# Roots on GpSimd, a sigmoid made of tanh, and one reciprocal for two softmax sums in a two-layer gated transformer kernel

## The chip, the cores and the metric

The kernel runs on one core of one Trainium2 chip. A core has five engines that run at the same time, each with its own in-order instruction stream: TensorE (PE, matrix products; its weight loads, PEld, are shown apart), VectorE (DVE), ScalarE (ACT, which evaluates functions such as exp from tables), GpSimd (POOL) and SyncE (SP, which issues DMAs). They wait for each other on semaphores. The metric is the device time of one execution in microseconds, the median of several runs. Lower is better.

## The reference

The input is x (4 batches, 512 rows, 512 columns) and a context (4, 512, 128). Four residual blocks follow one another, each gated by the tanh of a scalar. Cut to what matters here:

```python
# block 1: a learned adjacency, from the context
sim = einsum('bhnd,bhmd->bnm', Q, K) / (sqrt(32) * 4)
threshold = top_k(sim, 153)[0][:, :, -1:]
A = sigmoid(sim) * (sim >= threshold)
A = (A + swapaxes(A, -1, -2)) * 0.5
gamma = sigmoid(gamma_raw)
x = x + tanh(g_xattn[0]) * ((1 - gamma) * layernorm(x) + gamma * A)
# block 2: ternary weights, 8-bit activations, Hadamard rotations
x = x + tanh(g_ffn[0]) * down(silu(gate(layernorm(x))) * up(layernorm(x)))
# block 3: 16 heads, latent keys from the context, rotary positions
attn = softmax(scores); x = x + tanh(g_xattn[1]) * attention(layernorm(x), context)
# block 4: root-mean-square norm, ternary weights, 8-bit activations
x = x + tanh(g_ffn[1]) * (h + out(value * silu(gate)))   # h = layernorm(x)
```

where `layernorm(x) = (x - mean) / sqrt(var + 1e-5)` over the columns, without weights.

## The kernel before, in words

Everything is tiled to 128 partitions. A batch is four row tiles of 128x512 (`xs[b, j]`), an intermediate of the feed-forward blocks is 128x2048 a row tile. Matrix products of the attention are in fp32; the feed-forward products multiply bf16 activations with fp8 ternary weights.

**Adjacency (block 1, `adjacency`, lines 395 to 458).** For each of a batch's four row tiles, PE makes the similarities, ACT scales them into `sim` (line 420), and DVE finds the 153rd largest value of each row: 20 rounds of the eight largest (`max`, line 426), with `match_replace` (line 428) striking them out of `work` between rounds. ACT takes the sigmoid of `sim` (line 433), and one DVE instruction compares `sim` with the threshold and multiplies by the sigmoid (line 434). After the four tiles come the layer norm's statistics and the sum with the transpose (lines 437 to 458), scaled by `c_new`.

**Roots (`rsqrt_cols`, lines 147 to 159).** The reciprocal root of 128x4 variances (one column for each row tile): DVE adds epsilon, ACT takes the root (line 153), DVE takes the reciprocal (line 154), and four small DVE instructions make one Newton step. `ln_stats` calls it for the norms ahead of blocks 1, 2, 3 and 4 of each batch, and `feed1` once more for the root-mean-square norm: 20 calls.

**Feed-forward (`feed0`, `feed1`, `gated`, `tiles`, `projected`).** Silu on ACT (line 296), its product with the other half on DVE (line 297), Hadamard butterflies (DVE in line 513, GpSimd in line 481), quantization, transposes on PE with copies on ACT, and the product with the second weights (line 386). The weights are made ternary on ACT (`ternary`, lines 204 to 241: Abs with a sum, then Identity and Sign). The second layer's weights are made while attention runs.

**Attention (class `Pair`, lines 712 to 828).** 16 heads are worked two at a time: 8 pairs for each of 4 batches. `head` makes queries, `rope` rotates them (products with cosine and sine on DVE, lines 745 to 750, their sum on GpSimd, line 751), `rotated` projects them (line 708). `scores(j)` handles one block of 128 rows of both heads: two score matrices in PSUM (lines 781 and 784), and for each head the negated row maximum on DVE (line 789), Exp with its row sum on ACT (line 792), the reciprocal of the sum on DVE (line 794) and the product with it on ACT (line 795). The sums and reciprocals are 128x1 tiles. `turn(j)` transposes the result on PE (line 803) and copies it to `pT` on ACT (line 804). `attended` and `added` multiply with the values (line 811) and the output weights (line 823) and add to x (line 828). Within a pair, `scores(j)` goes out beside the next pair's queries and `turn(j - 2)`; the last two blocks are turned at the end of the pair. `hidden_T` (lines 671 to 681) makes the normalized, transposed hidden state at the start of a batch's attention.

**What sets the order.** The source interleaves generators. `attention` yields once a row block; between two yields, pieces of the next batch's adjacency and first feed-forward block, or of the second layer's weights and feed-forward, are issued according to their estimated costs (the numbers behind `yield`) and due times (`jobs`, lines 931 and 932). From that order and the dependencies, the framework places each instruction on its engine's stream: an instruction whose inputs are expected later can be overtaken by a later one of the source. On the chip each stream is then in order. Tiles take their places from rotating pools (`bufs`). In front of an ACT instruction whose function isn't in the table set that is active, a table load is put into ACT's stream; these loads carry the line of the instruction behind them.

At the start, batch 0's adjacency runs with the preparation of keys and output weights (`ahead`, whose DMAs to device memory are issued from POOL's queue, lines 647 and 667) and of the first layer's weights. At the end, the last feed-forward runs without attention beside it (`alone`).

Of the kernel before, what the change touches and what calls it, by code (L numbers as in the profile page):

```python
# [9 lines left out]
F32 = mybir.dt.float32  # L10
# [5 lines left out]
P = 128  # L16
# [17 lines left out]
def flamingo_kernel(  # L34
# [51 lines left out]
    def front_t(name):  # L86
        if mine("front", 2):
            return two_k("front", 3, name)
        return wp.tile([P, 512], F32, tag="pp", name=name, bufs=7)
# [22 lines left out]
    magic = const.tile([P, 2], F32, tag="magic", name="magic")  # L112
    nc.vector.memset(magic[:, 0:1], MAGIC)
    nc.vector.memset(magic[:, 1:2], -MAGIC)
    had_sb = const.tile([P, P], F32, tag="had", name="had_sb")
    nc.scalar.dma_start(had_sb, had)
    wqk = const.tile([P, 2, DC], F32, tag="wqk", name="wqk")
# [10 lines left out]
    nc.scalar.activation(gt, gx_raw[:, 0:4], AF.Tanh)  # L128
    tgx0, tgx1, tgf0, tgf1 = (gt[:, i : i + 1] for i in range(4))
    gam = const.tile([P, 1], F32, tag="gam", name="gam")  # L130
    nc.scalar.activation(gam, gx_raw[:, 4:5], AF.Sigmoid)

    c_keep = const.tile([P, 1], F32, tag="ck", name="c_keep")
    nc.vector.tensor_scalar(c_keep, gam, -1.0, 1.0, ALU.mult, ALU.add)
    nc.vector.tensor_tensor(c_keep, c_keep, tgx0, ALU.mult)
    c_new = const.tile([P, 1], F32, tag="cn", name="c_new")
    nc.vector.tensor_scalar(c_new, gam, 0.5, tgx0, ALU.mult, ALU.mult)

    def drain(gen):
        try:  # L140
# [6 lines left out]
    def rsqrt_cols(v, n, name):  # L147

        w = small.tile([P, n], F32, tag="rs_w", name=f"w_{name}")
        r = small.tile([P, n], F32, tag="rs_r", name=f"r_{name}")  # L150
        t = small.tile([P, n], F32, tag="rs_t", name=f"t_{name}")
        nc.vector.tensor_scalar(w, v, EPS, None, ALU.add)
        nc.scalar.activation(t, w, AF.Sqrt)
        nc.vector.reciprocal(r, t)
        nc.vector.tensor_tensor(t, r, r, ALU.mult)
        nc.vector.tensor_tensor(t, t, w, ALU.mult)
        nc.vector.tensor_scalar(t, t, -0.5, 1.5, ALU.mult, ALU.add)
        nc.vector.tensor_tensor(r, r, t, ALU.mult)
        return r
# [235 lines left out]
    def adjacency(b):  # L395
        cT = front_t(f"cT_{b}")
        nc.sync.dma_start(cT, cxT[:, b * S : (b + 1) * S])
        proj = []
        for i in range(2):
            pq = bg_ps(f"pq_{b}_{i}")  # L400
            nc.tensor.matmul(pq, wqk[:, i, :], cT, start=True, stop=True)
            t = bp.tile([P, S], F32, tag=f"qk{i}", name=f"qk{i}_{b}")
            nc.scalar.copy(t, pq)
            proj.append(t)
        qT, kT = proj
        if alone[0]:
            adj = hp.tile([P, NT, S], F32, tag="hT", name=f"adj_{b}", bufs=1)
        else:
            adj = big(f"adj_{b}").rearrange("p (j s) -> p j s", j=NT)
        for j in range(NT):  # L410
            if j == (0 if alone[0] else NT - 1):
                for k in range(NT):
                    t = xp.tile([P, D], F32, tag="x", name=f"x{b}_{k}")
                    nc.sync.dma_start(t, x[(b * NT + k) * P : (b * NT + k + 1) * P, :])
                    xs[b, k] = t
            i = f"{b}_{j}"
            psim = bg_ps(f"psim_{i}")
            nc.tensor.matmul(psim, qT[:, j * P : (j + 1) * P], kT, start=True, stop=True)
            sim = gate_t(f"sim_{i}")
            nc.scalar.activation(sim, psim, AF.Copy, scale=SIM_SCALE)  # L420
            work = back_t(f"work_{i}")
            cur = sim
            rounds = (TOPK + 7) // 8
            for r in range(rounds):
                m8 = small.tile([P, 8], F32, tag="m8", name=f"m8_{i}_{r}")
                nc.vector.max(m8, cur)  # L426
                if r < rounds - 1:
                    nc.vector.match_replace(work, m8, cur, GONE)  # L428
                    cur = work
                yield 1.45  # L430
            at = (TOPK - 1) % 8
            sg = front_t(f"sig_{i}")
            nc.scalar.activation(sg, sim, AF.Sigmoid)
            nc.vector.scalar_tensor_tensor(
                adj[:, j, :], sim, m8[:, at : at + 1], sg, ALU.is_ge, ALU.mult
            )
        mv, r = ln_stats([xs[b, j] for j in range(NT)], f"a{b}")

        kr = small.tile([P, NT], F32, tag="ckr", name=f"ckr_{b}")
        nc.vector.tensor_scalar(kr, r, c_keep, None, ALU.mult)  # L440
        km = small.tile([P, NT], F32, tag="ckm", name=f"ckm_{b}")
        nc.vector.tensor_tensor(km, kr, mv[:, :, 0], ALU.mult)
        nc.vector.tensor_scalar(kr, kr, 1.0, None, ALU.add)
        yield 5.0
        for j in range(NT):
            i = f"{b}_{j}"
            pt = psb.tile([P, 4, P], F32, tag="bg", name=f"padj_{i}")
            for k in range(NT):
                nc.tensor.transpose(pt[:, k, :], adj[:, k, j * P : (j + 1) * P], ident)
            nc.vector.tensor_scalar(  # L450
                xs[b, j], xs[b, j], kr[:, j : j + 1], km[:, j : j + 1], ALU.mult, ALU.subtract
            )
            sym = front_t(f"sym_{i}")
            nc.vector.tensor_tensor(sym, adj[:, j, :], pt.rearrange("p k q -> p (k q)"), ALU.add)
            nc.vector.scalar_tensor_tensor(
                xs[b, j], sym, c_new, xs[b, j], ALU.mult, ALU.add
            )
            yield 2.0
# [253 lines left out]
    class Pair:  # L712


        def __init__(self, b, g):
            self.b, self.g, self.u = b, g, f"{b}_{g}"
            self.qhs, self.ros, self.pps = [], [], {}

        def head(self, i):
            pq = mm_ps(f"pqh_{self.u}_{i}")  # L720
# [9 lines left out]
        def rope(self, i):  # L730


            both = []
            for o in range(2):
                pb = mm_ps(f"pb_{self.u}_{i}_{o}")
                at = (2 * i + o) * P
                nc.tensor.matmul(  # L737
                    pb, self.wc[:, at : at + P], self.qhs[i if i < 2 else o], start=True, stop=True
                )
                both.append(pb)  # L740
            for o in range(2):
                t = o if i < 2 else 2
                ro = wp.tile([P, S], F32, tag="ro", name=f"ro_{self.u}_{i}_{o}", bufs=7)
                rs = wp.tile([P, S], F32, tag="rs", name=f"rs_{self.u}_{i}_{o}", bufs=3)
                nc.vector.tensor_tensor(ro, both[o], cos_q[:, t, :], ALU.mult)  # L745
                if i < 2:
                    nc.vector.tensor_tensor(rs, both[1 - o], sin_q[:, t, :], ALU.mult)  # L747
                else:
                    for to, fro in ((slice(0, 64), slice(64, P)), (slice(64, P), slice(0, 64))):
                        nc.vector.tensor_tensor(rs[to, :], both[o][fro, :], sin_q[to, t, :], ALU.mult)  # L750
                nc.gpsimd.tensor_tensor(ro, ro, rs, ALU.add)  # L751
                self.ros.append(ro)

        def rotated(self):

            wr, ros, u = self.wr, self.ros, self.u
            self.kr = wp.tile([P, S], F32, tag="kr", name=f"kr_{u}", bufs=1)
            nc.sync.dma_start(self.kr, kr_d[self.b, self.g])
            pr = mm_ps(f"pr_{u}")
            for o in range(3):  # L760
                at = 2 * o * 64
                halves(
                    pr, (wr[:, at : at + 64], wr[:, at + 64 : at + P]),
                    (ros[o], ros[2 + o]) if o < 2 else (ros[4], ros[5]),
                    start=(o == 0), stop=(o == 2),
                )
            self.qr = wp.tile([P, S], F32, tag="qr", name=f"qr_{u}", bufs=1)
            nc.scalar.copy(self.qr, pr)
            self.pT = [
                wp.tile([P, NT, S], F32, tag="pT", name=f"pT_{u}_{i}") for i in range(2)  # L770
            ]

        def scores(self, j):

            pss = []
            for i in range(2):
# [5 lines left out]
                else:  # L782
                    with tc.high_priority():
                        nc.tensor.matmul(*args, start=True, stop=True)  # L784
                pss.append(p)
            for i in range(2):
                v = f"{self.u}_{i}_{j}"
                nm = small.tile([P, 1], F32, tag="nm", name=f"nm_{v}")
                nc.vector.tensor_reduce(nm, pss[i], AX.X, ALU.max, negate=True)  # L789
                pp = wp.tile([P, S], F32, tag="pp", name=f"pp_{v}", bufs=7)  # L790
                sm = small.tile([P, 1], F32, tag="sm", name=f"sm_{v}")
                nc.scalar.activation(pp, pss[i], AF.Exp, bias=nm, accum_out=sm)  # L792
                rs = small.tile([P, 1], F32, tag="rsm", name=f"rsm_{v}")
                nc.vector.reciprocal(rs, sm)  # L794
                nc.scalar.activation(pp, pp, AF.Copy, scale=rs)  # L795
                self.pps[i, j] = pp

        def turn(self, j):
            for i in range(2):
# [285 lines left out]
```

## Time and profile before

| | |
|---|---|
| median of 3 runs | 2125.17 us (2123.82 to 2126.85) |
| the profiled execution | 2130.4 us |
| its span, first to last instruction | 2128.6 us |
| mean granted TensorE clock | 0.975 |
| ACT table loads | 129, 1283 ns each: 57 before Exp, 42 before Silu, 18 before a root, 10 before the adjacency's sigmoid, 2 at the start |
| roots on ACT, line 153 | 20, about 0.21 us each |
| reciprocals of the softmax sums, line 794 | 256, 154 ns each |
| adds of the rotary halves on GpSimd, line 751 | 192, 1315 ns each |

How to read the profile: "busy" is the time an engine was executing, as a share of the span. In rows of groups, the numbers behind the first bar are the total busy time in us and the mean duration of one in ns; behind the second bar stands the engine's idle time just before these instructions, with what ended it. The chain of waits follows the work that ended last back to the start, at each step to what released it. In a timeline row, the first numbers are start and duration in us, and square brackets give idle time before it. In a row of windows, the stretch is followed by its length and the busy us (and instruction count) of PE, PEld, DVE, ACT and POOL, then the granted clock, the DMA share and GB/s.

### The profile page before, as it was taken

The numbers are of one execution on the slowest core, as the hardware profiler recorded it, in microseconds if no ns is written. First come the engines' busy times: TensorE is split into PE (matmuls) and PEld (weight loads), VectorE is DVE, ScalarE is ACT, GpSimd is POOL, SyncE is SP. The second block draws the span as 40 slices with busy tenths as digits, with TensorE's granted clock in tenths as the row PEclk, the third lists the DMA queues.
The fourth block names the chain that finished last, engine by engine and source line by source line (L and its number), as shares of the span: only waits on it lengthen the run. The fifth ranks groups of instructions, "written<-read, shape, count | busy, mean of one in ns | idle before, by whom it ended". The sixth has DMA issues, their size and how long they took to land.

```text
span 2128.6 us, 21689 instructions
## 1 busy us (share of the span) xinstructions
PE 1875.0 (88%) x7274; PEld 878.8 (41%) x7274; DVE 1620.9 (76%) x3203; ACT 1216.8 (57%) x1997; POOL 345.9 (16%) x332
## 2 busy tenths in 40 slices
PE   1259789999999989999989898999879999999898
PEld 0125534444454333444543333445433444444444
DVE  7987679997766999966669999676645756766775
ACT  6836535535555554456545544565599565676644
POOL 3032012113011111321111112210111210111000
PEclk9979989999999999999999999999999999999999
DMA  7452101111100211110012111011367111111000
GB/s 261 148 190 88 45 23 50 44 40 41 33 24 27 81 41 49 40 37 24 32 32 63 59 41 49 24 31 37 124 230 263 46 36 51 54 33 43 12 16 25
DMA packets 62175, 137.66 MB, mean 65 GB/s; under 512 B 7152, under 2 KB 14704, under 8 KB 58992
## 3 DMA queue, kind: packets, MB, share of 16 engines
q1 hardware_dynamic: 56592, 120.35, 18.0%
q0 software_dynamic: 4320, 14.16, 1.8%
q10 hardware_dynamic: 1152, 1.77, 0.2%
q8 instruction: 58, 0.95, 0.2%
q14 instruction: 53, 0.43, 0.1%
HBM read 116.33 MB, written 19.92 MB: 64 GB/s over the span
## 4 chain that ended last, share of the span: by engine, by line
PE 43%; DVE 38%; ACT 12%; issue 3%; DMA 2%; POOL 2%; SPq 0%; POOLq 0%; ACTq 0%; DVEq 0%
PE po L823 7%; DVE work L428 7%; DVE m L426 7%; PE pc L811 6%; PE pqh L722 4%; DVE nm L789 4%; DVE ro L745 3%; PE pzh_f L525 3%; DVE rs L750 3%; PE pu_g L291 2%; PE pd_g L386 2%; DVE rs L747 2%; PE pr L708 2%; PE pd_f L386 2%; PE pg_g L291 2%
## 5 line engine op out<-in xcount | busy, mean ns | idle before, releaser
L751 POOL TENSOR_TENSOR ro<-ro,rs 128x512 f32<-128x512 f32 x192 | 252.1, 1315 | 1400.9 <-DVE rs L747 962.6
L792 ACT ACTIVATE pp<-pss,nm 128x512 f32<-128x512 f32 x256 | 175.0, 687 | 222.5 <-DVE nm L789 221.8
L722 PE MATMUL pqh<-hT,wq 128*128 128x512 f32 x512 | 240.6, 611 | 6.4 <-ACT pp L792 4.3
L811 PE MATMUL pc<-pT,kv 128*128 128x512 f32 x512 | 240.0, 600 | 6.7 <-ACT pT L804 6.6
L823 PE MATMUL po<-om,cxo 128*128 128x512 f32 x512 | 231.0, 597 | 0.0
L789 DVE TENSOR_REDUCE nm<-pss 128x1 f32<-128x512 f32 x256 | 169.7, 680 | 69.2 <-PE pss L784 68.5
L426 DVE MAX8 m<-work 128x8 f32<-128x512 f32 x304 | 209.5, 689 | 4.5
L737 PE MATMUL pb<-qh,wc 128*128 128x512 f32 x384 | 193.2, 618 | 14.7 <-ACT qh L727 9.3
L795 ACT ACTIVATE pp<-pp,rsm 128x512 f32<-128x512 f32 x256 | 179.4, 723 | 32.2 <-DVE rsm L794 31.9
L428 DVE MATCH_REPLACE8 work<-m,work 128x512 f32<-128x512 f32 x288 | 194.5, 675 | 0.2
L804 ACT COPY pT<-ppt 128x512 f32<-128x512 f32 x256 | 141.8, 588 | 56.0 <-PE ppt L803 55.6
L803 PE MATMUL ppt<-ident,pp 128*128 128x128 f32 x1024 | 152.0, 282 | 11.2 <-ACT pT L804 7.8
L828 DVE SCALAR_TENSOR_TENSOR x<-po,gt,x 128x512 f32<-128x512 f32 x128 | 95.3, 746 | 82.5 <-PE po L823 81.5
L803 PEld LDWEIGHTS ppt<-ident,pp 128*128 128x128 f32 x1024 | 117.8, 143 | 96.3 <-issue 45.5
L722 PEld LDWEIGHTS pqh<-hT,wq 128*128 128x128 f32 x512 | 95.2, 194 | 133.2 <-issue 96.8
L781 PE MATMUL pss<-kr,qr 64*128 64x512 f32 x256 | 144.6, 645 | 5.8 <-ACT pp L792 5.0
L784 PE MATMUL pss<-kr,qr 64*128 64x512 f32 x256 | 145.6, 649 | 3.3 <-DVE x L828 1.8
L745 DVE TENSOR_TENSOR ro<-pb,cos_q 128x512 f32<-128x512 f32 x192 | 130.5, 680 | 14.8 <-PE pb L737 14.0
L823 PEld LDWEIGHTS po<-om,cxo 128*128 128x128 f32 x512 | 94.1, 190 | 114.3 <-issue 96.0
L811 PEld LDWEIGHTS pc<-pT,kv 128*128 128x128 f32 x512 | 90.8, 190 | 98.9 <-issue 85.3
L708 PE MATMUL pr<-ro,wr 128*64 128x512 f32 x192 | 96.5, 610 | 28.6 <-POOL ro L751 23.0
L737 PEld LDWEIGHTS pb<-qh,wc 128*128 128x128 f32 x384 | 66.0, 192 | 94.8 <-issue 37.7
(263 smaller groups left out, 3147.4 us busy)
## 6 DMA issues: line engine op xcount, KB each, us to landing
wq<-in_wqh SPq DMA_DIRECT2D x64, 256.0 KB, 2.6
om<-omd SPq DMA_DIRECT2D x64, 256.0 KB, 2.8
wc<-in_wkcq SPq DMA_DIRECT2D x32, 384.0 KB, 3.1
krd<-krs POOLq DMA_DIRECT2D x32, 256.0 KB, 2.3
kr<-krd SPq DMA_DIRECT2D x32, 256.0 KB, 2.6
sa_w1v<-in_gvT SPq DMA_DIRECT2D x8, 1024.0 KB, 5.6
sb_w1v<-in_gvT SPq DMA_DIRECT2D x8, 1024.0 KB, 5.3
wr<-in_wqr SPq DMA_DIRECT2D x32, 192.0 KB, 2.4
```

The costliest lines, as they stand in the source:

```text
L426: nc.vector.max(m8, cur)
L428: nc.vector.match_replace(work, m8, cur, GONE)
L722: nc.tensor.matmul(pq, self.wqs[i][:, c, :], hT[self.b][:, c, :], start=(c == 0), stop=(c == NC - 1),)
L737: nc.tensor.matmul(pb, self.wc[:, at : at + P], self.qhs[i if i < 2 else o], start=True, stop=True)
L745: nc.vector.tensor_tensor(ro, both[o], cos_q[:, t, :], ALU.mult)
L751: nc.gpsimd.tensor_tensor(ro, ro, rs, ALU.add)
L789: nc.vector.tensor_reduce(nm, pss[i], AX.X, ALU.max, negate=True)
L792: nc.scalar.activation(pp, pss[i], AF.Exp, bias=nm, accum_out=sm)
L795: nc.scalar.activation(pp, pp, AF.Copy, scale=rs)
L803: nc.tensor.transpose(pt[:, l, :], pp[:, l * P : (l + 1) * P], ident)
L811: nc.tensor.matmul(pc, kv[self.b][:, l, :], self.pT[i][:, l, :], start=(l == 0), stop=(l == NT - 1),)
L823: nc.tensor.matmul(po, self.cxo[i][:, j * P : (j + 1) * P], self.oms[i], start=(i == 0), stop=(i == 1),)
```

## The change

- In `rsqrt_cols`, ACT's root and DVE's reciprocal give way to one GpSimd instruction that raises w to the power of minus a half, with the exponent from a constant tile. The Newton step stays.
- The sigmoid of the adjacency becomes tanh of half the argument. sigmoid(s) = (1 + tanh(s/2)) / 2, and the adjacency is kept doubled: a DVE comparison writes the mask into `work`, and one DVE instruction makes (tanh + 1) times the mask. The factor of a half moves into `c_new` (0.25 for 0.5). The sigmoid of gamma is made of tanh in the same way, with one small DVE instruction.
- In `scores`, the two heads' sums go into two columns of one 128x2 tile, and one reciprocal serves both. It stands behind both Exps, and both products behind it.
- The rotated queries are kept in a dictionary by their numbers instead of a list, which changes no instruction.

```diff
+    power = const.tile([P, 4], F32, tag="mh", name="minus_half")
+    nc.vector.memset(power, -0.5)
...
-    nc.scalar.activation(gam, gx_raw[:, 4:5], AF.Sigmoid)
+    nc.scalar.activation(gam, gx_raw[:, 4:5], AF.Tanh, scale=0.5)
+    nc.vector.tensor_scalar(gam, gam, 0.5, 0.5, ALU.mult, ALU.add)
...
-    nc.vector.tensor_scalar(c_new, gam, 0.5, tgx0, ALU.mult, ALU.mult)
+    nc.vector.tensor_scalar(c_new, gam, 0.25, tgx0, ALU.mult, ALU.mult)
...
         nc.vector.tensor_scalar(w, v, EPS, None, ALU.add)
-        nc.scalar.activation(t, w, AF.Sqrt)
-        nc.vector.reciprocal(r, t)
+        nc.gpsimd.tensor_tensor(r, w, power[:, 0:n], ALU.pow)
         nc.vector.tensor_tensor(t, r, r, ALU.mult)
...
-            sg = front_t(f"sig_{i}")
-            nc.scalar.activation(sg, sim, AF.Sigmoid)
-            nc.vector.scalar_tensor_tensor(
-                adj[:, j, :], sim, m8[:, at : at + 1], sg, ALU.is_ge, ALU.mult
-            )
+            th = front_t(f"th_{i}")
+            nc.scalar.activation(th, sim, AF.Tanh, scale=0.5)
+            nc.vector.tensor_scalar(work, sim, m8[:, at : at + 1], None, ALU.is_ge)
+            nc.vector.scalar_tensor_tensor(adj[:, j, :], th, 1.0, work, ALU.add, ALU.mult)
...
+            sm = small.tile([P, 2], F32, tag="sm", name=f"sm_{self.u}_{j}")
+            rs = small.tile([P, 2], F32, tag="rsm", name=f"rsm_{self.u}_{j}")
             for i in range(2):
                 v = f"{self.u}_{i}_{j}"
                 nm = small.tile([P, 1], F32, tag="nm", name=f"nm_{v}")
                 nc.vector.tensor_reduce(nm, pss[i], AX.X, ALU.max, negate=True)
                 pp = wp.tile([P, S], F32, tag="pp", name=f"pp_{v}", bufs=7)
-                sm = small.tile([P, 1], F32, tag="sm", name=f"sm_{v}")
-                nc.scalar.activation(pp, pss[i], AF.Exp, bias=nm, accum_out=sm)
-                rs = small.tile([P, 1], F32, tag="rsm", name=f"rsm_{v}")
-                nc.vector.reciprocal(rs, sm)
-                nc.scalar.activation(pp, pp, AF.Copy, scale=rs)
+                nc.scalar.activation(pp, pss[i], AF.Exp, bias=nm, accum_out=sm[:, i : i + 1])
                 self.pps[i, j] = pp
+            nc.vector.reciprocal(rs, sm)
+            for i in range(2):
+                pp = self.pps[i, j]
+                nc.scalar.activation(pp, pp, AF.Copy, scale=rs[:, i : i + 1])
```

More of the change, by code (lines that the diff above doesn't have):

```diff
@@ L716, in __init__ @@
             self.b, self.g, self.u = b, g, f"{b}_{g}"
-            self.qhs, self.ros, self.pps = [], [], {}
+            self.qhs, self.ros, self.pps = [], {}, {}
         def head(self, i):
@@ L751, in rope @@
                 nc.gpsimd.tensor_tensor(ro, ro, rs, ALU.add)
-                self.ros.append(ro)
+                self.ros[i, o] = ro
         def rotated(self):
@@ L763, in rotated @@
                     pr, (wr[:, at : at + 64], wr[:, at + 64 : at + P]),
-                    (ros[o], ros[2 + o]) if o < 2 else (ros[4], ros[5]),
+                    (ros[0, o], ros[1, o]) if o < 2 else (ros[2, 0], ros[2, 1]),
                     start=(o == 0), stop=(o == 2),
```

## The prediction

> **What bounds the kernel now.** I read the page's busy times first, then busy time by stage (the windows view, at boundaries I chose: top-k of batch 0; its feed-forward; then, for each batch, a stage with the next batch's top-k and one with its feed-forward; the second layer's weights; the rest), and last the chain of waits.
>
> ```profile
> PE 1875.0 (88%) x7274; PEld 878.8 (41%) x7274; DVE 1620.9 (76%) x3203; ACT 1216.8 (57%) x1997; POOL 345.9 (16%) x332
> ...
> PE 43%; DVE 38%; ACT 12%; issue 3%; DMA 2%; POOL 2%; SPq 0%; POOLq 0%; ACTq 0%; DVEq 0%
> ```
>
> No one engine bounds it. ACT, where most of the change is, carries only 12% of the chain that ends last. By stage (columns: PE, PEld, DVE, ACT, POOL busy us):
>
> ```profile
> 700.00:890.00 190.00, 172.73 (x535) 72.88 (x532) 186.16 (x411) 93.07 (x176) 33.83 (x27) 1.00 0.18 54
> 890.00:1130.00 240.00, 229.59 (x980) 114.16 (x981) 162.79 (x273) 135.74 (x237) 41.59 (x38) 0.98 0.11 32
> ...
> 1550.00:1665.00 115.00, 98.75 (x311) 44.62 (x310) 57.75 (x133) 111.28 (x142) 18.63 (x15) 0.97 0.63 210
> ```
>
> Top-k stages are DVE's (186.2 of 190 us; likewise 155.3 of 160 at 320 and 185.7 of 190 at 1130), feed-forward stages PE's, and only the weights' stage is ACT's (111.3 of 115). So an ACT saving counts fully in 115 us, DVE's in some 540 us, and elsewhere only where a step stands alone. Groups of ACT and DVE that the change touches:
>
> ```profile
> L792 ACT ACT_TABLE_LOAD x57 | 73.1, 1283 | 0.9
> L296 ACT ACT_TABLE_LOAD x42 | 53.9, 1283 | 0.9 <-PE pg_g L291 0.2
> L153 ACT ACT_TABLE_LOAD x18 | 23.1, 1283 | 0.3
> L433 ACT ACT_TABLE_LOAD x10 | 12.8, 1283 | 0.2
> ...
> L794 DVE RECIPROCAL rsm<-sm 128x1 f32<-128x1 f32 x256 | 38.7, 154 | 28.9 <-ACT pp L792 28.3
> ```
>
> A step that stands alone, from the timeline at the start of batch 1's attention:
>
> ```profile
> 687.22 0.17 DVE L152 TENSOR_SCALAR w_q<-mv_q 128x4 f32<-128x4 f32 x1
> 688.06 1.28 ACT L153 ACT_TABLE_LOAD   x1
> 689.36 0.20 ACT L153 ACTIVATE t_q<-w_q 128x4 f32<-128x4 f32 x1
> 689.60 0.18 DVE L154 RECIPROCAL r_q<-t_q 128x4 f32<-128x4 f32 x1 [2.20 <-ACT t_q L153]
> 689.81 0.16 DVE L155 TENSOR_TENSOR t_q<-r_q 128x4 f32<-128x4 f32 x1
> ```
>
> DVE stands still 2.20 us for a root of 4 columns: ACT finishes a copy, loads a table, takes the root.
>
> **What the Trainium skill says.** "ScalarE: Activation LUTs", section "What ACT_TABLE_LOAD costs", gives about 1283 ns for a load plus 1380 ns of drain. The trace has the 1283 ns; no drain of that size shows (at 688.06 the load starts 0.02 us after the copy). Its section "Table sets: the hidden batching unit" puts exp and tanh in one set and sqrt in another. No tanh stands near an exp in this trace, so that the new tanh needs no load of its own beside the softmax rests on the page. "GPSIMD Engine Reference", section "3.1 Elementwise — side-by-side cycle accounting", gives 2.6 cycles an element for a two-input add as a software loop; the 128x512 add of line 751 takes 1315 ns, which agrees. It has no price for a power. "VectorE: DVE Perf Modes", "The perf-mode tier table", lets a one-input fp32 operation from SBUF run at twice a two-input one's rate; line 581 (479 ns) beside line 745 (680 ns) agrees.
>
> **The change, part by part**, against the profiled execution's 2130.4 us (span 2128.6). The median of the runs is 2125.17, or 0.9975 of it.
>
> *Table loads.* I listed ACT's Exp, Silu, Sqrt, Sigmoid and Tanh in order of time, struck out Sqrt, counted sigmoids as exp's set, and counted changes of set: 129 before, 80 after. The 49 that go are all 18 before a root, 9 of 10 before line 433, the one of line 131, and the reloads behind them (19 before exp, 2 before Silu): 49 x 1.283 = 62.9 us of ACT. Of these, 12 loads (15.1 us) lie on the chain; 21 of the others lie in the three DVE-bound stages and are worth nothing there.
>
> *The root on GpSimd.* 20 calls. Unknown: a power of 128x4. Low end 0.2 us: POOL's adds at 256 and 512 columns (about 740 and 1315 ns) extrapolate to about 0.17 us at 4, and a power is not cheaper than an add. High end 2.2 us: more than a 512-column add[...]; there the call costs what today's wait does. I take 1.0, plus two handovers (0.07 us DVE to POOL at line 751, 0.03 back): 1.1 us. Four calls stand alone on the chain; from the end of w to the first product behind the reciprocal they take 2.42 (687.39 to 689.81), 2.41 (at 1119), 2.99 (1552) and 2.30 us (1841), together 10.1. They become 4.4: **-5.7**. At 277 the chain runs over ACT through the second root's load and the root (1.28 + 0.20), which delay the copies of hT: **-1.5**. In the weights' stage ACT is full: the loads at 1568.0, 1647.0 and 1648.5 and a root, 3 x 1.283 + 0.20: **-4.1**. In the tail two roots sit between Silu calls, with loads at 2039.7, 2041.2, 2043.2 and 2044.7. The scale of line 566 waits for both: 6.3 us from 2039.84; two powers and the same small DVE steps make about 5, and Silu no longer stands ahead of line 566 at 2046.0 (0.6): **-1.9**. Elsewhere top-k or matmuls cover the call. POOL's queue: ahead of a call are line 751's adds (at most two, 1.3 us each, whose inputs DVE made earlier) and, in the opening, kv's rotation and the stores of om and kr, which wait up to 74 us for ACT. In before, batch 0's root is taken at 15 us, ahead of those stores; I expect the power there too, and the top-k to cover it. Behind a waiting power stand the next rope adds, for which PE waits at line 708, and line 481's butterflies, which need the root anyway.
>
> *Sigmoid out of tanh.* The tanh costs what the sigmoid did. DVE gets 16 comparisons 128x512, between 0.40 us (479 ns less the 0.08 that neighbours overlap) and 0.75 (no fast mode); taken 0.5. All but the first lie where DVE is the bound: **+8.0**. Batch 0's four also count, since DVE is on its chain. The handful of constants at the start: nothing, covered by the DMAs of x.
>
> *One reciprocal.* 128 of 256 go. One takes 154 ns but the next instruction starts 0.07 us after it. The chain holds 10.2 us of them; half: **-5.1**. Against it, both normalisations now wait for the second Exp:
>
> ```profile
> 717.10 0.21 ACT L792 ACTIVATION_READ_ACCUMULATOR pp<-pss,nm 128x1 f32 x1
> 717.20 0.73 ACT L795 ACTIVATE pp<-pp,rsm 128x512 f32<-128x512 f32 x1
> 718.12 0.72 ACT L795 ACTIVATE pp<-pp,rsm 128x512 f32<-128x512 f32 x1 [0.19 <-DVE rsm L794]
> ```
>
> Today the first head's product starts at once behind the second Exp's sum (0.10 us before the read's end in the median of 128 row blocks). Later it can't start sooner than 0.23 us after that end, the shortest way over DVE in the trace; in the median this way takes 1.16. ACT may do other copies meanwhile, and the products are turned two blocks later, except for a pair's last two. The first product is on the chain 19 times: 0 to 19 x 0.33 = 6; taken **+3**.
>
> *Loads off the chain* outside the DVE-bound stages: 16 x 1.283 = 20.5 us. What was behind them is next late, so I credit **-3**, and 0 to 14 as bounds.
>
> Sum: -5.7 - 1.5 - 4.1 - 1.9 + 8.0 - 5.1 + 3 - 3 = **-10.3**, so 2120.1 in the profiled execution, 2114.9 in the median: **2115 us**.
>
> **Rivals.** *More relief* (0.16): the 16 loads do hold back PE in the feed-forward stages, at the 14 us of their bound: 2115 - 11, and a power near 0.4 us takes another 3: 2101. For it: ACT is 57 to 60% busy there, and DVE waits 17.0 us in all at line 297 for Silu. Against: a PE near 96% has little idle time to give.
>
> *It cancels* (0.18): comparisons at 0.75 (+4) and a power at 1.7 us on some six calls (+4): 2123. For it: the comparison sits in the fullest DVE stages. Against: line 581's 479 ns.
>
> *The late normalisation decides* (0.14), slower. At the end of each of 32 pairs the last block's transposes and the copy of pT wait for both products, and the products for the one reciprocal behind whatever DVE is doing: 1.2 us later by the median way. At 24 pair ends that is 29 us against the 13.3 gained otherwise: 2125 + 15 = 2140. It is slower from about 15 of the 32. Against: the next pair's matmuls usually fill PE there.
>
> *It doesn't do what it says*: the instructions are placed anew, and if Exp and Silu alternate more often, some of the 49 loads come back; each such load costs at most 1.28 us, inside the ranges.
>
> **How the numbers follow.** Likeliest (0.52) 2115, its own range 2107 to 2121. A measurement of this kernel tells about 0.2% (4.3 us) from no change. Faster: 0.52 + 0.16 = 0.68; same 0.18; slower 0.14. The range reaches from 2097, under the relief case, to 2132, part of the way to the slower one.
>
> **What would show it.** Right: no load before roots or tanh-only stretches, about 80 in all; a wait of some 1.1 us in place of 2.2 at each hidden-state start; the weights' stage 4 us shorter; each top-k stage within 1 us. Wrong: a power over 2 us; over 90 loads; more idle time before line 795's products, with PE waiting for the transposes at pair ends.

## The result, and the profile after

The changed kernel took 2138.14 us (median of 6 runs, 2132.80 to 2143.48), the kernel before 2127.19 us in the same measurement (6 runs, 2123.82 to 2131.84). The ratio is 1.0047, 95% interval [1.0036, 1.0059]: **slower by about 10 us**. I had predicted 2115 us and a range of 2097 to 2132; the sign is wrong and the time lies outside. The profiled execution took 2139.34 us, its span is 2137.6. Lines of the changed kernel are 2 to 5 higher than those of before.

The page after, busy times and then the chain of waits by engine:

```profile
PE 1882.0 (88%) x7274; PEld 883.4 (41%) x7274; DVE 1611.8 (75%) x3073; ACT 1155.3 (54%) x1930; POOL 366.6 (17%) x352
...
DVE 43%; PE 43%; ACT 7%; issue 3%; POOL 2%; DMA 2%; SPq 0%; POOLq 0%; DVEq 0%; ACTq 0%
```

The change did what it says. ACT is 61.5 us less busy, POOL 20.7 us more, DVE has 130 instructions fewer. ACT's part of the chain fell from 12% to 7%, but DVE took over what ACT lost (38% to 43%). PE has the same 7274 matmuls, and was busy 7.0 us longer with them. The mean granted clock of this profile is 0.952, after 0.975, but that isn't the cause: of the other executions of the kernel before, those at 0.95 to 0.96 took 2128.7 us in the median and those at 0.97 to 0.98 took 2129.9. The loads, and the power as the groups of instructions show it (instructions, then busy us and mean ns):

```profile
L298 ACT ACT_TABLE_LOAD x41 | 52.6, 1283 | 0.9 <-PE pg_g L293 0.2
L795 ACT ACT_TABLE_LOAD x40 | 51.3, 1283 | 0.7
...
L437 DVE TENSOR_SCALAR work<-sim,m 128x512 f32<-128x512 f32 x16 | 7.6, 473 | 0.1
L156 POOL TENSOR_TENSOR r_q<-w_q,minus_half 128x4 f32<-128x4 f32 x4 | 4.1, 1022 | 129.0 <-DVE w_q L155 86.3 <-DVE w_a L155 42.8
```

There are 82 loads in all, after 129 (80 were forecast), and no load stands before a root or a tanh of the adjacency. A power of 128x4 takes 1.02 us, as estimated. The same stretches as before (PE, PEld, DVE, ACT, POOL busy us):

```profile
700.00:890.00 190.00, 176.89 (x537) 74.63 (x537) 186.35 (x397) 82.00 (x164) 34.04 (x27) 0.99 0.18 54
890.00:1130.00 240.00, 226.04 (x964) 111.84 (x963) 159.70 (x253) 130.00 (x231) 44.22 (x40) 0.97 0.11 31
...
1550.00:1665.00 115.00, 99.68 (x321) 44.32 (x320) 61.10 (x135) 106.11 (x135) 18.74 (x15) 0.97 0.68 232
```

ACT has 5 to 11 us less to do in each, and the work is no further on: 16 matmuls fewer have run in the 240 us of the feed-forward stage. The start of batch 1's attention, timeline of the changed kernel:

```profile
689.71 1.02 POOL L156 TENSOR_TENSOR r_q<-w_q,minus_half 128x4 f32<-128x4 f32 x1 [29.38 <-DVE w_q L155]
690.76 0.16 DVE L157 TENSOR_TENSOR t_q<-r_q 128x4 f32<-128x4 f32 x1 [1.13 <-POOL r_q L156]
...
697.46 0.69 DVE L428 MAX8 m<-sim 128x8 f32<-128x512 f32 x1 [3.99 <-ACT sim L422]
```

The wait for the root is 1.13 us where it was 2.20, as forecast. But 7 us later DVE waits 3.99 us for the scaled similarities. Before, its first MAX8 stood among the root's last small steps and didn't wait:

```profile
690.09 0.69 DVE L426 MAX8 m<-sim 128x8 f32<-128x512 f32 x1
```

And the waits view, which adds up all waits of one instruction for one releaser (us in total, times, longest). First before, then after:

```profile
ACT pp L795 <- DVE rsm L794: 31.9, 49, 2.5
...
PE ppt L803 <- ACT pT L804: 7.8, 22, 1.6
...
PE ppt L803 <- ACT pp L795: 2.6, 3, 2.1
```

```profile
ACT pp L800 <- DVE rsm L797: 54.0, 81, 3.5
...
PE ppt L807 <- ACT pp L800: 18.2, 19, 3.9
...
PE ppt L807 <- ACT pT L808: 5.6, 15, 1.0
```

The normalisations wait for their reciprocal more often, and PE stands before the transposes for a normalised block 18.2 us in place of 2.6; its wait for a copy of `pT` is no longer (5.6 after 7.8). Of the 18.2 us, 14.9 fall on the last row block of 11 of the 32 pairs of heads: nine of these waits are of 1.1 us, all of them in the top-k stages. This was named as the sign of the slower rival.

### The profile page after: what moved, and what is told of

It reads as the page before. It is cut to its first block, busy times and chain, and to the rows that moved or that the text cites. A ratio compares the mean times of both kernels' runs of the same rounds, so it can differ in the third digit from the quotient of the medians.

```text
span 2137.6 us, 21521 instructions
## 1 busy us (share of the span) xinstructions
PE 1882.0 (88%) x7274; PEld 883.4 (41%) x7274; DVE 1611.8 (75%) x3073; ACT 1155.3 (54%) x1930; POOL 366.6 (17%) x352
## 4 chain that ended last, share of the span: by engine, by line
DVE 43%; PE 43%; ACT 7%; issue 3%; POOL 2%; DMA 2%; SPq 0%; POOLq 0%; DVEq 0%; ACTq 0%
DVE work L430 9%; DVE m L428 9%; PE pc L815 6%; PE po L827 5%; PE pqh L724 4%; DVE nm L793 4%; PE pb L739 3%; PE pzh_f L527 3%; DVE ro L747 3%; DVE rs L752 3%; PE pu_g L293 2%; PE pss L783 2%; PE pd_f L388 2%; PE pu_f L293 2%; DVE x L832 2%
## 5 line engine op out<-in xcount | busy, mean ns | idle before, releaser
L753 POOL TENSOR_TENSOR ro<-ro,rs 128x512 f32<-128x512 f32 x192 | 251.6, 1312 | 1226.3 <-DVE rs L749 937.1
L800 ACT ACTIVATE pp<-pp,rsm 128x512 f32<-128x512 f32 x256 | 171.7, 720 | 55.8 <-DVE rsm L797 54.0
L807 PE MATMUL ppt<-ident,pp 128*128 128x128 f32 x1024 | 151.4, 282 | 23.9 <-ACT pp L800 18.2
L710 PE MATMUL pr<-ro,wr 128*64 128x512 f32 x192 | 98.9, 619 | 23.2 <-POOL ro L753 15.6
```

Source lines behind the costliest of these rows:

```text
L807: nc.tensor.transpose(pt[:, l, :], pp[:, l * P : (l + 1) * P], ident)
```

## The experiments

The runs first take the parts of the change apart, then ask what the loads and the order of the instructions are worth (the framework places the instructions anew for every program, by an estimate of each one's time), and last what the late normalisation costs by itself. What each theory expected stands with each run. Ratios are to the kernel before, measured beside each kernel; a ratio's part over 1 times 2129 us gives the microseconds.

### One part of the change at a time

**e1_one_recip**: only the single reciprocal. **e2_pow**: only the roots. **e3_tanh**: only the tanh. **e4_pow_tanh**: the change without the single reciprocal.

```diff
 e1: +nc.vector.reciprocal(rs, sm)   # 128x2, after both Exp; two products follow
 e2: +nc.gpsimd.tensor_tensor(r, w, power[:, 0:n], ALU.pow)
 e3: +nc.scalar.activation(th, sim, AF.Tanh, scale=0.5)
     +nc.vector.tensor_scalar(work, sim, m8[:, at : at + 1], None, ALU.is_ge)
     +nc.vector.scalar_tensor_tensor(adj[:, j, :], th, 1.0, work, ALU.add, ALU.mult)
 e4: e2 and e3
```

> Only the one reciprocal for two sums; roots and sigmoid as before. Theory (late normalisation: both products wait for the second Exp and for DVE, and PE waits for the transposes): slower than before by 12 to 22 us, ratio 1.006 to 1.010, with PE's and PEld's wait for the products before line 803's transposes about twice the 13 us of before. Rival (the small parts, root and sigmoid, lose the time): within 5 us of before or faster by up to 5.

> Only the roots on GpSimd. Theory (late normalisation): faster by 8 to 14 us, since 18 loads before roots and most of the reloads behind them go. Rival (the roots' new place or the new placing of instructions loses it): no faster than before, 0 to 10 us slower.

> Only the sigmoid made of tanh, roots still on ACT. Theory (late normalisation): slower by 0 to 8 us, the 16 comparisons on DVE less the loads before line 433. Rival (the comparison carries the loss): slower by 10 us or more.

> The change without its one reciprocal: roots on GpSimd and the sigmoid made of tanh. Theory (late normalisation): faster than before by 3 to 10 us (ratio 0.995 to 0.9985). Rival (root or sigmoid lose it): slower than before by 5 us or more, near the changed kernel's 1.0047.

Measured: e1 1.0089 [1.0075, 1.0103], e2 1.0009 [1.0001, 1.0017], e3 1.0034 [1.0020, 1.0048], e4 1.0043 [1.0030, 1.0057]. No part gains. The single reciprocal costs 19 us alone, yet 1 us between e4 and the whole change: the parts don't add up, so something besides their own work is at play. The roots alone take away 31 table loads (129 to 98) and gain nothing: +2 us. Where a gain was expected (e2, e4), the rival came in; e1 and e3 lie where their theories put them.

### Is it the loads or the order?

**e5_free_loads, e7_placed_1000, e8_placed_1200** leave the kernel before as it is and change only the time that the framework puts down for a table load when it places the instructions: 0, 1000 and 1200 ns. **e10_after_1000, e11_after_1200** do the same to the changed kernel. **e6_free_loads_one_set** is e5 with functions that need no other table.

```diff
+hw_specs.TRN2Spec.ACT_TABLE_LOAD_NS = 0       # e5, e6; 1000 in e7, e10; 1200 in e8, e11
 e6 too:
-nc.scalar.activation(t, w, AF.Sqrt)
+nc.scalar.activation(t, w, AF.Copy)
-nc.scalar.activation(sg, sim, AF.Sigmoid)
+nc.scalar.activation(sg, sim, AF.Tanh)
```

> The kernel before with the same instructions, but placed on the engines' streams as if a table load cost nothing (the framework's estimate for it set to 0), so that its order no longer depends on which function a step uses. 108 loads in the program instead of 129. It is the base for the next kernel. Theory (what the change gains or loses is mostly where instructions land): 5 to 15 us away from before, either way. Rival (loads and waits themselves decide): within 4 us, a little faster for 21 loads fewer.

> The same placing rule, but ACT's root is replaced by a plain copy and the sigmoid by a tanh (the layer norms' factors and the adjacency's values are not the reference's), so that 48 loads go while nearly all instructions keep their order. Theory (loads off the chain are worth nothing and those on it nearly their length): 8 to 16 us faster than the kernel with free loads. Rival (removing loads is worth nothing here, since the next wait is as late): within 4 us of it.

> The kernel before, with the same instructions and the estimate for a table load at 1000 ns instead of 1283: a change of nothing but the order in which instructions are placed, about as far from before's order as the root and tanh parts are. Theory (placing alone moves the time by as much as the change did): 4 to 12 us away from before. Rival (placing is neutral): within 4 us.

> As the kernel placed at 1000 ns, with 1200 ns: a smaller change of order alone. Theory (placing): 2 to 10 us away from before. Rival (placing is neutral): within 4 us.

> The changed kernel with the same instructions, placed with a table load at 1000 ns. Theory (before's order is a lucky one among many; other orders cost before 7 to 19 us): 2120 to 2150 us, that is faster than the kernel before placed at 1000 (2148). Rival (the change costs time of itself): at or above the kernel before placed at 1000, 2148 or more.

> The changed kernel placed with a table load at 1200 ns. Theory (placing): 2120 to 2145 us, on average with the 1000 ns placing below before's two placed kernels (2148 and 2136). Rival (the change costs time of itself): 2140 or more.

Measured: e5 1.0191 [1.0177, 1.0205], e6 1.0043 [1.0031, 1.0056], e7 1.0081 [1.0067, 1.0095], e8 1.0027 [1.0015, 1.0038], e10 1.0077 [1.0062, 1.0092], e11 1.0047 [1.0033, 1.0060]. The same instructions in another order (with the loads that this order needs: 108 in e5, 134 in e7, 128 in e8) cost 6 to 41 us: the order of the kernel before is the best of the four tried. In nearly e5's order (132 of PE's 7274 places and 38 of ACT's 1868 hold another instruction in e6), 48 loads fewer (108 to 60) go with 31 us less; in the chain of waits the loads' part fell from 67.7 to 28.2 us. That is twice what e6's theory gave at most, and e5 and e7 moved further than theirs. With 1000 ns the changed kernel takes 1 us less than the kernel before placed alike (5 by the medians), with 1200 ns 4 us more (1 by the medians), each known to some 4 us, where it took 10 more at 1283. So a new placing can cost more than the whole change moves, and what the change or a load is worth depends on it.

**e9_same_order** shows what the loads are worth in the order of before: the functions are exchanged after the instructions are placed (roots and sigmoid are then not computed), so every engine keeps its order.

```diff
+swap = {AF.Sqrt: AF.Copy, AF.Sigmoid: AF.Tanh}
+        if isinstance(ins, mybir.InstActivation) and ins.func in swap:
+            block.instructions[at] = copy.replace(ins, func=swap[ins.func])
```

> The kernel before in exactly its own order on every engine: only after all instructions were placed, ACT's root was turned into a copy and its sigmoid into a tanh (layer norms and adjacency values are not the reference's), so that 49 of the 129 loads fall away and nothing else moves. Theory (loads were worth what the prediction said, and the new placing takes it back): 11 to 20 us faster than before. Rival (in before's own order the loads are hidden): within 4 us of before.

Measured: 0.9982 [0.9974, 0.9990], 2124.86 us, with 80 loads. So 49 loads fewer are worth 4 us here. In the chain of waits the loads' part fell from 43.3 to 28.2 us, by just the 15.1 us that I had read off, and the time didn't follow. The trace shows where the rest goes. From the end of the last pair of heads to the end of the span it takes 85.8 us, before 89.7: the tail gives 3.9 us, about all of the gain. At the start of batch 1's attention (e9's timeline):

```profile
687.91 0.18 DVE L154 RECIPROCAL r_q<-t_q 128x4 f32<-128x4 f32 x1 [0.79 <-ACT t_q L153]
...
688.99 0.60 ACT L420 ACTIVATE sim<-psim 128x512 f32<-128x512 f32 x1 [1.11 <-PE psim L418]
...
689.62 0.69 DVE L426 MAX8 m<-sim 128x8 f32<-128x512 f32 x1 [1.14 <-ACT sim L420]
```

Without the load the root's wait is 0.79 us in place of 2.20. But the next large instruction in DVE's order is MAX8, which needs `sim`, and ACT gets `psim` from PE only now: MAX8 waits 1.14 us. It began at 690.09 before and at 689.62 here, when e9 was already 0.27 us ahead (`w_q` at 686.95 after 687.22): of 1.41 us, 0.2 are left. Two of the other three such calls gave PE no more (0.2 us at 1119, nothing at 1841); the one at 1552 gave it 1.4 us, in the stage of the second layer's weights. In that stage, from 1553 to 1590 us, before and then in e9:

```profile
1553.00:1590.00 37.00, 29.17 (x105) 14.87 (x106) 16.70 (x38) 34.95 (x48) 7.62 (x6) 0.91 0.61 205
```

```profile
1553.00:1590.00 37.00, 31.07 (x105) 15.77 (x106) 16.45 (x38) 33.08 (x46) 7.61 (x6) 0.86 0.61 208
```

ACT has 1.9 us less to do, but PE takes 1.9 us longer for the same 105 matmuls, at a granted clock of 0.86 in place of 0.91. The pair of heads that ends at 1603.8 us before ends 0.2 us earlier in e9. But the missing loads needn't be what lowered the clock. The kernel of e13 (below) has before's order and before's loads up to the tail, and its profile shows the same:

```profile
1553.00:1590.00 37.00, 31.23 (x107) 15.66 (x108) 16.79 (x38) 34.79 (x46) 7.61 (x6) 0.88 0.57 193
```

Between 1585 and 1590 us e13 falls back by 1.0 us against before, and e9 by 1.1. So two profiles of one order can differ by this much, and what the 1.4 us would have come to at before's clock isn't shown.

**e13_tail_pow** takes the power only for the tail, where the loads did count; what stands ahead keeps its order.

```diff
+if name in (f"g{B - 1}", f"rms{B - 1}"):
+    nc.gpsimd.tensor_tensor(r, w, power[:, 0:n], ALU.pow)
+else:
     nc.scalar.activation(t, w, AF.Sqrt)
     nc.vector.reciprocal(r, t)
```

> The kernel before with the root on GpSimd only in the last feed-forward (its layer norm and its root-mean-square norm), so that the order of all instructions ahead is before's own. Theory (loads count where nothing else is as late, which is the tail): 2 to 4 us faster than before, all of it behind 2039 us. Rival (hidden too): within 1 us.

Measured: 0.9988 [0.9981, 0.9996], 2126.66 us where the kernel before took 2129.15. This version beats both kernels, by 2.5 us over the one before (0.9 to 4.0 by the interval). Its tail, from the trace:

```profile
2037.26 1.04 POOL L156 TENSOR_TENSOR r_g<-w_g,minus_half 128x4 f32<-128x4 f32 x1 [76.62 <-DVE w_g L154]
...
2039.79 1.01 POOL L156 TENSOR_TENSOR r_rms<-w_rms,minus_half 128x4 f32<-128x4 f32 x1 [1.49 <-DVE w_rms L154]
...
2042.03 1.52 ACT L571 ACTIVATE n_g<-x,gc 128x512 f32<-128x512 f32 x2 [1.59 <-DVE gc L564]
```

The scale that waits for both roots (line 571 here, 566 before) starts 6.0 us after the last pair's end (2036.0), before 7.7 us (2046.59 after 2038.9).

### The comparisons

**e12_one_on_act** keeps e4 but makes the sigmoid's double on ACT, with one more ACT instruction a row tile, so that DVE keeps its one instruction. **e14_act_one_recip** is e12 with the single reciprocal.

```diff
 nc.scalar.activation(sg, sim, AF.Tanh, scale=0.5)
+nc.scalar.activation(sg, sg, AF.Identity, bias=ones[:, 0:1])
```

> Roots on GpSimd, two reciprocals as before, and the sigmoid made of tanh with the added one on ACT (one more ACT pass over 128x512 for each of 16 tiles), so that DVE keeps its single instruction. Theory (the comparisons cost DVE 6 to 8 us in the DVE-bound stages): 2 us faster to 3 us slower than before, 5 to 9 us faster than roots and tanh with the comparison (1.0043). Rival (placing explains that kernel's loss, not the comparison): about 1.004 again.

> Roots on GpSimd, tanh with the one added on ACT, and the one reciprocal for two sums. Theory (the late normalisation costs of itself): slower than its partner without it (1.0004) by 5 us or more, with PE's idle time before the transposes about 24 us against 11.7. Rival (the 19 us of the one reciprocal alone were placing): within 4 us of its partner.

Measured: e12 1.0004 [0.9995, 1.0014], e14 1.0025 [1.0018, 1.0032]. With e4 and the whole change this is a square of four kernels, in us over the kernel before: two reciprocals and the one on ACT +0.9, one reciprocal +5.3; with the comparison on DVE +9.2 and +10.0. So the kernels with the comparisons take 8.3 us more beside two reciprocals and 4.7 beside one. Each of the four has its own placing, so that this difference holds the placing too. The roots and the table loads (80 in e12), which I had counted as the gain, leave nothing: +0.9 us, with 11.6 us more of ACT for the added one.

### The single reciprocal

**e15_recip_1000** and **e16_recip_1200** add the single reciprocal to e7 and e8.

```diff
+hw_specs.TRN2Spec.ACT_TABLE_LOAD_NS = 1000    # e15; 1200 in e16
+nc.vector.reciprocal(rs, sm)                  # 128x2, as in e1
```

> The kernel before with the one reciprocal, placed with a table load at 1000 ns. Theory (costs of itself): 5 us or more above its partner, before placed at 1000 (1.0081), so 1.0105 or more. Rival (placing): 1.004 to 1.010.

> The kernel before with the one reciprocal, placed with a table load at 1200 ns. Theory (costs of itself): 5 us or more above its partner, before placed at 1200 (1.0027), so 1.005 or more. Rival (placing): 0.999 to 1.0046.

Measured: 1.0098 [1.0084, 1.0112] and 1.0071 [1.0058, 1.0083]. Over the kernels placed alike that is +4 us (e15 over e7) and +9 us (e16 over e8). With e1 (+19), e14 over e12 (+4) and the whole change over e4 (+1) there are five pairs: never the gain that I counted. Two of the five (e15 over e7, and the whole change over e4) are within the 4 us to which such a difference is known, and e15 came in at its rival where e16 came in at its theory, so that these pairs don't settle the size. PE's idle time before the transposes is 21 to 32 us in the kernels with one reciprocal, 11 to 16 in those with two.

What stayed open was whether the late start costs by itself or only through the new order. **e17_late_norm** and **e18_one_on_act_late** move the wait alone, in before and in e12: after placing, the first head's product gets the semaphore value of the second head's reciprocal. Nothing else differs, not even one instruction's place.

```diff
 for the product of head 0, where it stands behind the second Exp on ACT:
+waits = [copy.replace(w, wait_value=max(w.wait_value, at_of[other])) ...]
+block.instructions[at] = copy.replace(ins, sync_info=copy.replace(ins.sync_info, on_wait=waits))
```

> The kernel before with its own instructions in its own order on every engine; the only difference is the wait of the first head's normalisation (line 795), which in 102 of the 128 row blocks waits for the second head's reciprocal instead of its own (in the other 26 it stands ahead of the second Exp on ACT and keeps its own wait). All 256 reciprocals stay. So the late start is charged alone, without a new placing and without the DVE time that one reciprocal saves. Theory (the late start itself stalls PE at the transposes): +4 to +9 us, with PE's idle time before line 803's transposes up from 11.2 us to 18 or more. Rival (the late start is covered, and the loss in the kernels with one reciprocal comes from their new placing): within 2 us of before, PE's idle time before the transposes below 14 us.

> The kernel with roots on GpSimd, tanh with the one added on ScalarE, and two reciprocals (e12_one_on_act), in its own order, with the same edit of the wait alone (101 of 128 row blocks). e12_one_on_act took 1.0004 of before, and the same kernel with one reciprocal, placed anew, 1.0025. Theory (late start): 1.002 to 1.004, PE's idle time before the transposes up from 11.7 us to 18 or more. Rival (new placing): 1.000 to 1.001, idle time below 14 us.

Measured: e17 1.0078 [1.0063, 1.0093], 2144.01 us; e18 1.0080 [1.0066, 1.0095], 2146.06 us. **The wait alone costs 16 to 17 us** (e17 0.0078, e18 0.0080 less e12's 0.0004, times 2129; each known to some 4 us), nearly twice what the theory gave it at most. PE's idle time before the transposes is 26.5 us in e17 and 30.1 in e18. The waits view of e17, for the lines shown above of before:

```profile
ACT pp L795 <- DVE rsm L794: 80.8, 106, 2.4
...
PE ppt L803 <- ACT pT L804: 14.6, 24, 1.6
...
PE ppt L803 <- ACT pp L795: 10.9, 12, 2.1
```

ACT waits 49 us more for reciprocals. PE waits for the normalised block 8 us more, and for the copy of the turned blocks, `pT`, 14.6 us where the page before had 7.8. The second is new in e17 and e18 (19.4 us, after 8.5 in e12). In the seven kernels with one reciprocal, all placed anew, the wait for `pT` is only 4.5 to 7.3 us and the one for the normalised block 15.9 to 23.2: the late start reaches PE on both ways, and the order decides which. One block of e17, DVE, ACT and PE in order of time:

```profile
755.00 0.14 DVE L794 RECIPROCAL rsm<-sm 128x1 f32<-128x1 f32 x1
755.06 0.67 DVE L745 TENSOR_TENSOR ro<-pb,cos_q 128x512 f32<-128x512 f32 x1
755.10 0.19 ACT L792 ACTIVATION_READ_ACCUMULATOR pp<-pss,nm 128x1 f32 x1
...
755.72 0.67 DVE L428 MATCH_REPLACE8 work<-m,work 128x512 f32<-128x512 f32 x1
...
756.31 0.15 DVE L794 RECIPROCAL rsm<-sm 128x1 f32<-128x1 f32 x1
...
756.50 0.72 ACT L795 ACTIVATE pp<-pp,rsm 128x512 f32<-128x512 f32 x1 [1.20 <-DVE rsm L794]
...
757.12 1.05 ACT L804 COPY pT<-ppt 128x512 f32<-128x512 f32 x2
...
757.74 0.31 PEld L803 LDWEIGHTS ppt<-ident,pp 128*128 128x128 f32 x3 [2.10 <-ACT pT L804]
```

Read it from the bottom. PE waits 2.10 us for a copy of `pT`, to have a free buffer. The copy's input has long been there, but ACT works in order, and ahead of it stands the first head's product, which waits 1.20 us for the second reciprocal. DVE could have made that at 755.3, when the second sum was read, but has a rope product and a MATCH_REPLACE ahead of it. In the kernel before the same product starts at 752.37, beside the read's end, the same copy at 752.99, and PE waits 0.79 us there:

```profile
752.37 0.71 ACT L795 ACTIVATE pp<-pp,rsm 128x512 f32<-128x512 f32 x1
...
753.61 0.91 PEld L803 LDWEIGHTS ppt<-ident,pp 128*128 128x128 f32 x8 [0.79 <-ACT pT L804]
```

I set every matmul of e17 against the same one of before. The delay grows at the transposes by 17.6 us in all (and shrinks and grows at others), of which 5.9 in the second row block of a pair of heads and 9.2 in the last. From 922 us to 1113, in the feed-forward stage, it doesn't grow (6.8 us at both ends); over the top-k stage before it, from 737 to 922, it grows from 2.8 to 6.8. Of the 14 us between 320 us and the last pair's end, about half (7.1) falls in the three stages in which DVE is full, and 2.9 from 1545 to 1688 us, in the weights' stage, in which ACT is.

## Why the prediction was wrong

Against -10.3 us forecast stand +10 us. Two steps failed: savings that were read off the chain of waits (-12.8 us) were worth about nothing in before's order, and the late start of the normalisation, priced at 3 us, cost 16 to 17 in that same order. By the prediction's own steps:

**Loads counted: right.** 129 became 82; 80 were forecast, and e9 and e12 have 80. That tanh and exp share a table set, which I took from the Trainium skill ("ScalarE: Activation LUTs", section "Table sets: the hidden batching unit"), shows in the changed kernel's trace: ACT goes from one to the other 18 times without a load. The one load between a tanh and an exp (at 310.5 us) stands where two tanhs had followed a Silu, without a load of their own.

**"Four calls stand alone on the chain ... -5.7": the step that failed first.** The price was right (1.02 us for a power, 1.0 taken), the wait shrank as forecast (2.20 to 1.13 us), and the worth was wrong. A chain tells what ended last, not how much earlier the next wait would have ended. In e9 the loads of all four calls are gone and each wait is 1.4 us shorter, and of the one at batch 1 0.2 us remain, because `sim` comes nearly as late from PE. The same holds for **"In the weights' stage ACT is full ... -4.1"**: over the three pairs from 1545.0 to 1687.8 us, which take in all of its loads, it took 142.8 us before, 144.1 after (1554.0 to 1698.1), 142.1 in e9, and 143.0 in e13, where nothing is changed up to the tail: some 1 us at most for the loads, by these profiles. **"Loads off the chain ... -3"** had nothing behind it that shows: e9's gain is its tail's. Together, these three steps, -12.8 in my sum, were worth about nothing in before's order.

**At 277 us, -1.5: not told apart.** From 277 to 300 us e9 gains 2.7 us on before, after an opening that ran 2.4 us later; but e13, with nothing changed there, gains 2.6.

**The tail, -1.9: right, a little small.** From the last pair's end to the end of the span: 89.7 us before, 87.3 after, 86.4 in e13.

**Comparisons, +8.0: right in size of the work, not shown by itself.** 0.469 us for the comparison, and 0.680 in place of 0.734 for the instruction behind it: 16 x 0.415 = 6.6 us of DVE. The pairs of kernels differ by 8.3 and 4.7 us, placing included.

**"One reciprocal ... -5.1" and "taken +3": the second step that failed.** Alone, the late start costs 16 to 17 us at an unchanged order. I wrote that "ACT may do other copies meanwhile". In e17 it doesn't: those copies stand behind the waiting product on ACT, and PE waits for them. The +3 came from counting only where the product itself was on the chain, 19 times; in the changed kernel PE waits for products 15.6 us more than before. In the kernels placed anew the single reciprocal as a whole costs 1 to 19 us; the new orders hide some of the wait, or add to it. How much the fewer reciprocals gain on DVE wasn't measured by itself.

**The rival "The late normalisation decides"** gave 2140 us; 2138.14 were measured. Its mechanism is in the changed kernel's trace as it was written: PE stands at the end of a pair, mostly 1.1 us at a time (1.2 were priced), but at 11 pairs and not 24, so for 14.9 us (2.9 before) where I had priced 29. At an unchanged order (e17) the same late start costs 16 to 17 us, there also by way of `pT` in a pair's second row block. That the time agrees is partly chance: the rival's other half, 13.3 us gained elsewhere, didn't come. I held it unlikely because "the next pair's matmuls usually fill PE there", which fails beside a top-k: ten of the 11 ends lie there.

**"It doesn't do what it says"** looked for loads that come back. It left out the order: e7 and e8 show 6 to 17 us for the same instructions placed otherwise, and I had charged the new placing with loads only.

What stays open: with the loads at nothing, the tail at -1.9, the comparisons at +8.0, the late start at +17 and the fewer reciprocals at my unmeasured -5.1, the sum is +18, and +10 was measured; nor is it known why the comparisons and the single reciprocal together cost less (10.0 us) than one after the other (0.9 + 4.4 + 8.3); the orders differ on several engines at once, and I couldn't hold one fixed while the instructions change. What the placing gives or takes in the changed kernel is not measured by itself.

## What to carry to other kernels

A wait on the chain is worth only the distance to the next wait behind it in the same in-order queue: look up what the engine runs next and when its inputs come, before crediting the whole wait. A wait that is added can cost what is queued behind it: waiting for the second of two small operations, as joining them does, made ACT's products and copies late, and PE behind them, for 16 to 17 us at an unchanged order. And where a framework places the instructions, test an edit at the old order too (exchange a function, or a wait's value, after placing), for a new order alone moved this kernel by 6 to 41 us. And read a second profile of the same order, where there is one, before explaining a difference of 1 to 3 us between two traces.

## What the runs showed of the hardware that I had not expected

- A power of 128x4 on GpSimd takes 0.997 to 1.04 us in 17 of the changed kernel's 20 calls (1.44 in three of those for the root-mean-square norm), where its add of 128x512, with 128 times the elements, takes 1312 ns.
- A DVE instruction that compares a 128x512 tile with a column and multiplies by a second tile took 734 ns; one that adds a constant to a tile and multiplies by a second, 680 ns. Which of the differences makes the 54 ns wasn't tested.
- A tanh that followed a Silu needed no table load (at 286 us of the changed kernel), nor did one that followed an exp; from Silu to exp there was always a load.
- From 1553 to 1590 us, 105 to 107 matmuls of the same order kept PE busy for 29.2, 31.1 and 31.2 us in three profiles (before, e9, e13), at granted clocks of 0.91, 0.86 and 0.88; before and e13 have the same instructions there.
